# A gated feed-forward layer through tanh instead of SiLU, with a new order of the flow's steps

## The chip, the core and the metric

The kernel runs on one core of one Trainium2 chip. The metric is the time on the device in microseconds (us) of one execution; the figure for the kernel before is the median of three runs. A core has five engines that run at the same time and meet only at semaphores: PE (matrix multiplication, with a separate row for its weight loads), DVE (elementwise work and reductions), ACT (activation functions, copies, scaling), POOL (elementwise work and index-driven transfers) and SP, which here only issues transfers. Each engine works through its own instructions in the order in which the program gives them. PE writes to PSUM, a small memory of eight banks; DVE and ACT can read PSUM, POOL can't.

## What is computed

Eight batches of 512 tokens with 128 features pass through eight layers of attention, each followed by a feed-forward layer. The first half has experts that are chosen per token. The last four pairs of layers are the flow (called "stream" in the code) that this change touches: two attention layers and a feed-forward layer of kind `l2f`, twice, then the same with `l3f`; the last attention layer is a "hybrid" with a small router. Cut to what the change touches:

```
def ffn(x, w_gate, w_up, w_down):            # _L2_ffn_ref and _L3_ffn_ref
    gate = fp4_linear(x, w_gate)
    y = fp4_linear(x, w_up)
    h = jax.nn.silu(gate) * y
    return fp4_linear(h, w_down)             # h is quantised in blocks of 16

# in _L3_attn_b_ref
    logits = jax.nn.silu(route_in @ router_w1) @ router_w2 + router_b2
```

Here silu(g) = g * sigmoid(g). The hidden width of this layer is 352. Every other attention layer of the flow is causal softmax attention with 16 heads of 8 features; the softmax is taken with ACT's Exp.

## The kernel before

**The flow.** `stream` runs the four pairs of layers over eight batches, so 32 passes, numbered v = 0 to 31; pass v belongs to layer v // 8 and batch v % 8. The work of a pass is cut into steps with short names. Their order is one long written-out list of 237 entries, `STREAM`. An entry such as `V0:5` means: in round i, do step V0 of pass i - 5. So each round works on up to seven passes at once, each in another phase. `in_order` (L1806 and after) walks the list once per round; it leaves one empty place between the causal layers and the hybrid ones, and there are 32 + 1 + 6 = 39 rounds, the first and last ones only partly filled. A step that a pass does not have (the hybrid steps H, I, J, K in a causal layer, the steps m, x, w in a hybrid one) is left out. The kernel is built with manual scheduling: the instructions of each engine stand in the order in which the steps issue them, and a step issues to several engines.

**The feed-forward steps** are in `ffn_parts`. F0 to F8 normalise, quantise and transpose the input. V0 and V1 each compute the gates of two tiles of 128 tokens (L1382) into `ps`, a pair of PSUM banks from the pool `p_sc` with tag `sc`. S0 and S1 apply SiLU to such a pair on ACT (L1398) and write `sg` to SBUF. U0 to U3 compute the "up" product of one tile (L1382 again) into one bank. y0 to y3 multiply (L1407, DVE): h = sg * up, 128 x 352. z, D, C, A, M with a number quantise h: `scales` is a reduction and three short DVE instructions (L2420 to L2427), `divide` is on POOL, `cut` on ACT, `put` two dependent DVE instructions (L2446, L2447) for tiles 0 and 2 and three POOL instructions for tiles 1 and 3, `multiply` on POOL. n0 to n3 transpose h (L1415), N0 to N3 multiply with the down weights (L1424), E0 to E3 add to x (L1428).

**What shares the buffers.** `p_sc` has two pairs of banks. The attention scores take them too: each step x of `exp_parts` allocates a pair, has four (or two) matmuls written to it (L1093) and an Exp on ACT (L1103) that reads it; there are 24 such steps in a causal pass. In a hybrid pass the steps Ka to Kc use the pairs. The pool `p_b` has four single banks, for everything else: "up", the row-maximum products `mx` of the m steps (L1009, L1012, reduced on DVE in L1024), transposes, accumulators, the reduction result `amax`.

**Activation tables.** ACT evaluates Exp, SiLU, Gelu and Sqrt from tables; before an activation whose function is not in the set that is loaded stands an ACT_TABLE_LOAD. In the flow of the kernel before, such loads stand before L1398 (SiLU) and before the next Exp, in the causal layers L1103 and in the hybrid ones L1645 or others, and before the router's SiLU (L1537).

**The router** of the hybrid layer is in `hybrid_parts`: He (`route`) writes two small products into one bank, Hf (`hidden`) applies SiLU to 64 values on ACT, Hg (`at_landmarks`) reads the other part of the bank on DVE, Hh (`logits`) is a matmul of the hidden values, Hi (`biased`) adds the bias on DVE.

Of the kernel before, what the change touches and what calls it, by code (L numbers as in the profile page):

```python
# [25 lines left out]
AF = mybir.ActivationFunctionType  # L26
ALU = mybir.AluOpType
# [3 lines left out]
B, S, D, H, HD = 8, 512, 128, 16, 8  # L31
NT = S // P
EXPERTS, HID = 8, 512
FF = 352
# [48 lines left out]
class Net:  # L83
# [1094 lines left out]
    def stream(self, layers, back):  # L1178
# [3 lines left out]
        nc, a = self.nc, self.a  # L1182
        tile_pool = self.tc.tile_pool
        with tile_pool(name="flow_fix", bufs=1) as fix, tile_pool(name="flow", bufs=2) as pool, tile_pool(
# [182 lines left out]
            def ffn_parts(v, w, rows, cols, ffn_w, rope, eps, post):  # L1367

                b, box = v % B, {}
                gu, dn = ffn_w[:, 0 : 2 * FF], ffn_w[:, 2 * FF : 2 * FF + 3 * P].rearrange("p (c n) -> p c n", c=3)  # L1370
                xn = self.xnb(b)
                stats, shift, apply = self.norm_three(xn, self.xb(b))
                q = self.quantize_part(pool, xn.rearrange("p t d -> p (t d)"), S, "qx", 1)

                def turn():
                    box["xT"] = pool.tile([P, S], F32, tag="xT", name="xT", bufs=3)
                    self.transposed(box["xT"], xn, act=True)

                parts = {f"F{k}": f for k, f in enumerate((stats, shift, apply) + q + (turn,))}

                def wide(k, t, out):
                    nc.tensor.matmul(  # L1382
                        out[:, 0:FF],
                        lhsT=box["xT"][:, t * P : (t + 1) * P],
                        rhs=gu[:, k * FF : (k + 1) * FF],
                        start=True,
                        stop=True,
                    )


                def gates(i):
                    ps = box["ps", i] = self.sc()
                    for j in range(2):
                        wide(0, 2 * i + j, ps[:, j, :])

                def silu(i):
                    sg = box["sg", i] = pool.tile([P, 2, FF], F32, tag="sg", name="sg")
                    nc.scalar.activation(sg, box.pop(("ps", i))[:, :, 0:FF], AF.Silu)  # L1398

                def up(t):  # L1400
                    ps = box["up", t] = self.bank("up")
                    wide(1, t, ps)

                def product(t):
                    h = box["h", t] = pool.tile([P, FF], F32, tag="h", name="h", bufs=3)
                    sg = box["sg", t // 2][:, t % 2, :]
                    nc.vector.tensor_tensor(h, sg, box.pop(("up", t))[:, 0:FF], ALU.mult)  # L1407
                    box["q", t] = self.quantize_part(pool, h, FF, "qh", 2, t in (1, 3))

                def narrow_turn(t):  # L1410
                    h = box.pop(("h", t))
                    hT = box["hT", t] = pool.tile([P, 3, P], F32, tag="hT", name="hT")
                    pt = self.bank("m")
                    for c, (at, r) in enumerate(CH):
                        nc.tensor.transpose(pt[0:r, c * P : (c + 1) * P], h[:, at : at + r], self.ident)  # L1415
                    nc.scalar.copy(hT[:, 0:2, :], pt[:, 0 : 2 * P].rearrange("p (c n) -> p c n", c=2))
                    r = CH[2][1]
                    nc.scalar.copy(hT[0:r, 2, :], pt[0:r, 2 * P : 3 * P])

                def narrow(t):  # L1420
                    hT = box.pop(("hT", t))
                    o = box["o", t] = self.bank("av")
                    for c, (_, r) in enumerate(CH):
                        nc.tensor.matmul(o[:, 0:P], lhsT=hT[0:r, c, :], rhs=dn[0:r, c, :], start=c == 0, stop=c == 2)  # L1424

                def add(t):
                    x = self.xb(b)[:, t, :]
                    nc.vector.tensor_tensor(x, x, box.pop(("o", t))[:, 0:P], ALU.add)  # L1428
# [52 lines left out]
    def hybrid_parts(self, pool, b, weights, rows):  # L1481


        nc = self.nc
# [5 lines left out]
        wo, land, r2 = w[:, 929:1057], w[0:64, 1057:1185], w[0:64, 1185:1188]  # L1490
        scale = 32**-0.5
        xn = self.xnb(b)
        box, tiles = {}, {}
        stats, shift, apply = self.norm_three(xn, self.xb(b))

        def small(n, tag, bufs=2):
            return pool.tile([P, n], F32, tag=tag, name=tag, bufs=bufs)
# [28 lines left out]
            nc.vector.tensor_reduce(box["route"], box["xT"], AX.X, ALU.add)  # L1526

        def route():
            ps = box["r"] = self.bank("m")
            nc.tensor.matmul(ps[0:64, 0:1], lhsT=r1, rhs=box.pop("route"), start=True, stop=True)  # L1530
            nc.tensor.matmul(
                ps[0:1, 64:128], lhsT=box["xT"][:, S - 1 : S], rhs=landT, start=True, stop=True, skip_group_check=True
            )

        def hidden():
            hid = box["hid"] = small(1, "hhid")
            nc.scalar.activation(hid[0:64], box["r"][0:64, 0:1], AF.Silu, scale=1.0 / S)  # L1537

        def at_landmarks():

            t = box["at"] = small(72, "hat")
            nc.vector.tensor_copy(t[0:1, 0:64], box["r"][0:1, 64:128])
            nc.vector.tensor_reduce(t[0:1, 64:65], t[0:1, 0:64], AX.X, ALU.max, negate=True)
            nc.vector.tensor_scalar(t[0:1, 64:65], t[0:1, 64:65], D**-0.5, None, ALU.mult)

        def logits():
            ps = box["r"] = self.bank("m")
            nc.tensor.matmul(ps[0:1, 0:3], lhsT=box.pop("hid")[0:64], rhs=r2, start=True, stop=True)

        def biased():  # L1550
            t = box["lg"] = small(8, "hlg")
            nc.vector.tensor_tensor(t[0:1, 0:3], box.pop("r")[0:1, 0:3], rows[0:1, 256:259], ALU.add)
            nc.vector.tensor_reduce(t[0:1, 4:5], t[0:1, 0:3], AX.X, ALU.max, negate=True)

        def exponentials():
# [203 lines left out]


    STREAM = """
        Kd0:3 n2:6 x312:4 E1:6 Jc:4 m302:3 m220:3 x302:4 Jd:4 F5:5 t2:4 pv:2 d2:4 m221:3 Ka2:3 sk:2 x000:3 Ie:2
        F6:5 F7:5 m301:3 mg:1 x012:3 Je:4 M3:6 Ib:2 w3:4 m312:3 c3:4 m311:3 rv:2 x111:3 m320:3 Ke0:3 He:2 Kc3:3
        x010:3 m332:3 Kb2:3 Jf:4 t3:4 d3:4 st:1 Kf0:3 F8:5 N2:6 m321:3 Hk:3 m300:3 x011:3 Kd1:3 V0:5 Kc2:3 Hl:3
        Hg:2 E2:6 Jg:4 Hf:2 m330:3 m201:3 Hm:3 S0:5 Jh:4 aT:4 m200:3 sh:1 U1:5 n3:6 Kd2:3 Kd3:3 Ke1:3 g1 x001:3
        Kf1:3 x002:3 y1:5 U0:5 z1:5 y0:5 m231:3 l1:2 po:4 z0:5 N3:6 ap:1 Ka0:2 Jk:4 m322:3 E3:6 Ke2:3 bi:4 D1:5
        If:2 o0:4 Hn:3 D0:5 x101:3 Hh:2 m310:3 m210:3 l0:2 f1:3 x100:3 Ha:1 m110:2 o1:4 Ho:3 w0:3 C1:5 C0:5 h1:3
        m122:2 c0:3 V1:5 i1:3 A0:5 m112:2 Ji:4 A1:5 m131:2 m101:2 g0 S1:5 o2:4 T:1 Kb0:2 m130:2 Kf2:3 U2:5 y2:5
        Ke3:3 t0:3 o3:4 Ic:2 z2:5 Jj:4 Kc0:2 Hb:1 d0:3 M0:5 Jl:4 o4:4 x112:3 m111:2 ad:4 pq:1 m000:2 x110:3 D2:5
        l2:2 m020:2 pk:1 Hi:2 Ka3:2 Id:2 rq:1 m132:2 x102:3 M1:5 Pq:1 rk:1 U3:5 l3:2 Kf3:3 x201:3 Jm:4 Rq:1  # L1770
        m022:2 m030:2 x200:3 F0:4 y3:5 n0:5 w1:3 z3:5 C2:5 D3:5 c1:3 x210:3 A2:5 m002:2 x202:3 m031:2 M2:5 Ka1:2
        m011:2 n1:5 Hc:1 m032:2 x211:3 x212:3 m102:2 C3:5 m021:2 F1:4 sq:1 m100:2 Kb1:2 N0:5 A3:5 E0:5 F2:4
        m010:2 x300:3 m012:2 x301:3 Kb3:2 Hj:2 m212:2 m121:2 m001:2 Pk:1 m120:2 f0:2 t1:3 w2:3 d1:3 Rk:1 h0:2
        F3:4 m230:2 c2:3 i0:2 Hd:1 x310:3 m211:2 Ja:3 F4:4 Ia:1 Jb:3 x311:3 Kc1:2 m222:2 m331:2 m202:2 N1:5
        m232:2
# [913 lines left out]
```

## Time and profile before

| what | value |
|---|---|
| median of three runs | 3313.77 us (3310.12 to 3315.57) |
| the profiled execution | 3321.43 us, of this the core's span 3319.6 us |
| mean granted TensorE clock | 0.923 |
| ACT_TABLE_LOAD in the trace | 138, each 1283 ns |
| SiLU in the feed-forward layers (L1398) | 64 instructions of 128 x 704, 756 ns mean |
| product h = sg * up (L1407) | 128 instructions of 128 x 352 |
| Exp of the scores (L1103) | 832 instructions, 923 ns mean |
| from 1740.0 to 1838.2 us (flow fills) | 98.2 us; PE busy 88.55, DVE 78.70, ACT 62.46 |
| from 1838.2 to 2858.7 us (20 full causal rounds) | 1020.5 us, some 51 us each |
| from 2858.7 to 3052.3 us (change to the hybrid layer) | 193.6 us; PE busy 164.01, DVE 154.31, ACT 137.17 |
| from 3052.3 to 3319.6 us (hybrid rounds and the end) | 267.3 us |

The stages were taken from the start of the first SiLU (1838.2 us), which begins the feed-forward work of pass 0, and of every second one after it. Times inside the trace are in us from the start of the span. In the profile, lines of a group give: source line, engine, operation, output <- input, shapes, count, then busy time in us and the mean of one instruction in ns, then the idle time of the engine just before such instructions and what ended it. In the list of stages each engine has its busy time in us and, in brackets, its number of instructions; PEclk is the granted clock. The chain of waits is one path through the trace, followed back from the last instruction: at each step to what released the instruction, or to the one before it on its engine. A line of it has start, length, engine, tile and source line. ACT with a line and no tile is there a table load. Matmuls overlap one another and their ends are modelled, so a PE that is 98% busy may still have room.

### The profile page before, as it was taken

The page shows a single profiled execution, that of the slowest core. Times are in us where ns is not written, and L with a number is a line of the kernel's source. Part 1 is how long each engine was busy: PE and PEld are TensorE (multiplying, and loading weights), DVE is VectorE, ACT ScalarE, POOL GpSimd, SP SyncE. Part 2 cuts the span into 40 slices and gives each one's busy share as a digit, 9 for nine tenths or more (in the row PEclk, how much of TensorE's full clock was granted, in tenths as well). Part 3 has the DMA queues.
Part 4 walks back from the last instruction along what each step waited for, and adds up shares of the span by engine and source line. Part 5 has one row for each costly group of instructions (what it writes and reads, how often), then busy time and mean ns, then how long its engine had stood idle before and what let it go on. Part 6 is the DMA issues. An engine that isn't in the chain of part 4 may idle for free.

```text
span 3319.6 us, 65455 instructions
## 1 busy us (share of the span) xinstructions
PE 2823.0 (85%) x21824; PEld 1887.0 (57%) x21824; DVE 2521.8 (76%) x6837; ACT 2112.6 (64%) x4192; POOL 1852.6 (56%) x2476
## 2 busy tenths in 40 slices
PE   7783899999795867788748999999999999888886
PEld 4582753333295757767725566665656666555554
DVE  7844768998545696475337999989899999778895
ACT  5533478787643543566416778888888788676663
POOL 3355623431155652553335886677787777576676
PEclk9986999999897978899869999999999999998898
DMA  2023322221022300221232221111211111100000
GB/s 89 13 64 79 98 56 66 65 65 55 8 68 59 114 26 23 68 56 50 59 103 79 68 71 70 65 67 66 74 63 63 63 66 65 63 2 1 7 7 13
DMA packets 134774, 187.36 MB, mean 56 GB/s; under 512 B 20292, under 2 KB 103364, under 8 KB 134444
## 3 DMA queue, kind: packets, MB, share of 16 engines
q1 hardware_dynamic: 118348, 150.46, 13.6%
q0 software_dynamic: 14080, 28.86, 4.2%
q10 hardware_dynamic: 2016, 3.85, 0.5%
q8 instruction: 181, 2.97, 0.4%
q14 instruction: 149, 1.22, 0.1%
HBM read 128.81 MB, written 54.30 MB: 55 GB/s over the span
## 4 chain that ended last, share of the span: by engine, by line
PE 50%; DVE 28%; ACT 6%; DMA 6%; issue 5%; POOL 4%; SPq 1%; DVEq 0%; ACTq 0%; POOLq 0%
PE sc L826 6%; PE av L843 6%; PE av L1124 6%; PE mx L1012 6%; PE sc L1093 6%; DVE pm L1024 4%; DMA k<-d 3%; DVE nm L1031 2%; DVE bnst L205 2%; DVE bnmv L206 2%; PE m L1227 2%; PE av L1424 2%; ACT e L1103 2%; PE mx L1009 2%; PE sc L1382 1%
## 5 line engine op out<-in xcount | busy, mean ns | idle before, releaser
L1103 ACT ACTIVATE e<-sc 128x1024 f32<-128x1024 f32 (+1 forms) x832 | 739.3, 923 | 172.0 <-PE sc L1093 101.7
L1024 DVE TENSOR_REDUCE pm<-mx 128x4 f32<-128x512 f32 (+1 forms) x1152 | 629.6, 595 | 93.7 <-PE mx L1012 89.0
L1012 PE MATMUL mx<-k,q 126*128 126x512 bf16 (+3 forms) x2048 | 547.3, 321 | 44.5 <-DMA k<-d 34.9
L1093 PE MATMUL sc<-q,k 128*128 128x512 bf16 (+3 forms) x2048 | 446.4, 320 | 10.6 <-ACT e L1103 8.2
L1106 POOL TENSOR_SCALAR_AFFINE_SELECT e<-e 128x256 f32<-128x256 f32 x768 | 298.5, 409 | 205.7 <-ACT e L1103 201.0
L1124 PE MATMUL av<-e,vaug 128*32 128x512 f32 (+3 forms) x4096 | 369.1, 482 | 1.3 <-ACT e L1103 0.8
L1031 DVE TENSOR_REDUCE nm<-mx 128x1 f32<-128x512 f32 x512 | 329.2, 684 | 46.0 <-PE mx L1012 44.2
L806 POOL DMA_INDIRECT xg<-xd,srci x248 | 243.6, 982 | 211.7 <-DVE srci L799 107.2
L1012 PEld LDWEIGHTS <-q 126*128 126x128 bf16 x2048 | 197.6, 98 | 247.9 <-issue 167.8
L843 PE MATMUL av<-moe_w,h 128*128 x1984 | 266.9, 278 | 15.0 <-ACT xgT L820 4.5
L826 PE MATMUL sc<-xgT,w1c 128*128 128x128 f32 x1984 | 276.8, 285 | 2.4 <-ACT e L1103 2.4
L1009 PE MATMUL mx<-maskbf,identbf 128*128 128x128 bf16 (+1 forms) x1152 | 265.8, 238 | 10.0 <-DVE pm L1024 6.7
L892 POOL DMA_INDIRECT got<-yd,posi x192 | 199.8, 1041 | 133.1 <-issue 56.5
L826 PEld LDWEIGHTS sc<-xgT,w1c 128*128 128x128 f32 x1984 | 256.4, 201 | 14.5 <-ACT e L1103 4.6
L1093 PEld LDWEIGHTS <-k 128*128 128x128 bf16 x2048 | 183.1, 98 | 139.6 <-issue 56.8
L843 PEld LDWEIGHTS av<-moe_w,h 128*128 128x128 f32 x1984 | 243.1, 193 | 27.6 <-issue 8.0
L187 POOL TENSOR_SCALAR rstd<-bnmv 128x4 f32<-128x4 f32 x152 | 48.3, 318 | 373.8 <-DVE bnmv L206 365.6
L251 ACT ACTIVATE xn<-x,ln_shift,rstd 128x128 f32<-128x128 f32 x480 | 197.9, 489 | 67.0 <-DVE ln_shift L246 67.0
L814 DVE COPY w1c<-moe_w 128x516 f32 x248 | 117.2, 473 | 129.4 <-issue 32.4
L1124 PEld LDWEIGHTS av<-e,vaug 128*32 128x32 f32 x4096 | 107.7, 110 | 172.1 <-issue 145.4
L829 ACT ACTIVATE h<-sc 128x512 f32<-128x512 f32 x156 | 93.2, 598 | 166.0 <-PE sc L826 161.2
L262 PE MATMUL m<-ident,xn 128*128 128x128 f32 x480 | 85.4, 297 | 95.0 <-ACT xn L251 67.9
(427 smaller groups left out, 6386.7 us busy)
## 6 DMA issues: line engine op xcount, KB each, us to landing
q<-d SPq DMA_DIRECT2D x128, 288.0 KB
k<-d SPq DMA_DIRECT2D x384, 96.0 KB
d<-thirds SPq DMA_DIRECT2D x48, 384.0 KB
yd<-y SPq DMA_DIRECT2D x248, 64.0 KB
xd<-xn SPq DMA_DIRECT2D x32, 256.0 KB
d<-thirds SPq DMA_DIRECT2D x48, 128.0 KB
moe_w<-in_moe_w SPq DMA_DIRECT2D x8, 516.0 KB
moe_w<-in_moe_w SPq DMA_DIRECT2D x8, 512.0 KB
```

The costliest lines, as they stand in the source:

```text
L806: nc.gpsimd.indirect_dma_start(xg[i], None, s["xd"], bass.IndirectOffsetOnAxis(ap=srci[:, i : i + 1], axis=0))
L826: nc.tensor.matmul(ps[:, cols], lhsT=w1c[i][:, cols], rhs=xgT[i], start=True, stop=True)
L843: nc.tensor.matmul(ps[:, 0:P], lhsT=hid[i][:, c * P : (c + 1) * P], rhs=w2[:, bass.ds(e + c * P, P)], start=c == 0, stop=c == 3,)
L892: nc.gpsimd.indirect_dma_start(got[b][k][:, i, :], None, s["yd"], bass.IndirectOffsetOnAxis(ap=s["posi"][:, j : j + 1], axis=0))
L1009: nc.tensor.matmul(out, lhsT=self.identbf, rhs=mask, start=True, stop=False, skip_group_check=True)
L1012: nc.tensor.matmul(s[:, col : col + n], lhsT=q[:, t, :], rhs=key[:, 0 : n // P, :], start=not causal, stop=True, skip_group_check=True,)
L1024: nc.vector.tensor_reduce(box["pm"][:, h, at : at + n // P], s[:, 0:n].rearrange("p (k n) -> p k n", n=P), AX.X, ALU.max,)
L1031: nc.vector.tensor_reduce(box["nm"][:, u, h : h + 1], s, AX.X, ALU.max, negate=True)
L1093: nc.tensor.matmul(s[:, jj, col : col + n], lhsT=key[:, t, :], rhs=q[:, at // P : (at + n) // P, :], start=True, stop=True,)
L1103: nc.scalar.activation(e, s[:, :, 0:wide], AF.Exp, scale=scale)
L1106: nc.gpsimd.affine_select(out=e[:, :, col : col + P], in_=e[:, :, col : col + P], pattern=[[0, 2], [1, P]], compare_op=ALU.is_ge, fill=0.0 ...
L1124: nc.tensor.matmul(acc[g][32 * j : 32 * j + 32, at : at + n], lhsT=vaug[:, t, first : first + 32], rhs=pair[j // 2][:, j % 2, col : col + ...
```

## The change

Three things, all in the flow.

1. The gate. sigmoid(g) = (1 + tanh(g/2)) / 2, so silu(g) * u = (1 + tanh(g/2)) * u * g / 2. S0 and S1 now write tanh(g/2). The product step has two DVE instructions in place of one: h = (sg + 1) * up, then h = (h * 0.5) * gate, where gate is the PSUM pair of step V. The second reads what the first wrote. The PSUM pair was last read by S before; now it is last read by the second product of the odd tile, so by y1 or y3.
2. The router. `hidden` writes tanh of half the mean, `logits` has a DVE instruction of 64 x 1 ahead of its matmul that makes (1 + tanh) * g, and `biased` scales by 0.5/S while it adds the bias. The bank that `route` writes is named `r0` and is read by `logits` too.
3. The list STREAM is a new one: the same steps in another sequence, some with another lag (`E1:6` becomes `E1:5`, `Kd0:3` becomes `Kd0:2`, `mg:1` becomes `mg`, among others). The largest lag is 6 in both, so there are 39 rounds in both.

```diff
                 def silu(i):
                     sg = box["sg", i] = pool.tile([P, 2, FF], F32, tag="sg", name="sg")
-                    nc.scalar.activation(sg, box.pop(("ps", i))[:, :, 0:FF], AF.Silu)
+                    nc.scalar.activation(sg, box["ps", i][:, :, 0:FF], AF.Tanh, scale=0.5)
...
                     sg = box["sg", t // 2][:, t % 2, :]
-                    nc.vector.tensor_tensor(h, sg, box.pop(("up", t))[:, 0:FF], ALU.mult)
+                    gate = box["ps", t // 2][:, t % 2, 0:FF]
+                    nc.vector.scalar_tensor_tensor(h, sg, 1.0, box.pop(("up", t))[:, 0:FF], ALU.add, ALU.mult)
+                    nc.vector.scalar_tensor_tensor(h, h, 0.5, gate, ALU.mult, ALU.mult)
+                    if t % 2:
+                        del box["ps", t // 2]
...
-            ps = box["r"] = self.bank("m")
+            ps = box["r0"] = self.bank("m")
...
-            nc.scalar.activation(hid[0:64], box["r"][0:64, 0:1], AF.Silu, scale=1.0 / S)
+            nc.scalar.activation(hid[0:64], box["r0"][0:64, 0:1], AF.Tanh, scale=0.5 / S)
...
         def logits():
+            hid = box.pop("hid")
+            nc.vector.scalar_tensor_tensor(hid[0:64], hid[0:64], 1.0, box["r0"][0:64, 0:1], ALU.add, ALU.mult)
             ps = box["r"] = self.bank("m")
-            nc.tensor.matmul(ps[0:1, 0:3], lhsT=box.pop("hid")[0:64], rhs=r2, start=True, stop=True)
+            nc.tensor.matmul(ps[0:1, 0:3], lhsT=hid[0:64], rhs=r2, start=True, stop=True)
...
-            nc.vector.tensor_tensor(t[0:1, 0:3], box.pop("r")[0:1, 0:3], rows[0:1, 256:259], ALU.add)
+            logit = box.pop("r")[0:1, 0:3]
+            nc.vector.scalar_tensor_tensor(t[0:1, 0:3], logit, 0.5 / S, rows[0:1, 256:259], ALU.mult, ALU.add)
```

Of the list, the stretch around the gates, first as it was and then as it is:

```
... N2:6 m321:3 Hk:3 m300:3 x011:3 Kd1:3 V0:5 Kc2:3 Hl:3 Hg:2 E2:6 Jg:4 Hf:2 m330:3 m201:3 Hm:3 S0:5 Jh:4 aT:4
    m200:3 sh:1 U1:5 n3:6 Kd2:3 Kd3:3 Ke1:3 g1 x001:3 Kf1:3 x002:3 y1:5 U0:5 z1:5 y0:5 ...

... rv:2 m312:3 Ib:2 Ke0:3 Kf0:3 V0:5 m331:3 S0:5 m321:3 Hd:2 Kd2:3 x002:3 sh:1 He:2 U0:5 aT:4 Jg:4 x111:3 U1:5
    Kc3:3 If:2 y0:5 z0:5 y1:5 Jh:4 Ke1:3 po:4 Ka0:2 Ke2:3 D0:5 Hf:2 Jk:4 bi:4 z1:5 o0:4 V1:5 ...
    ... S1:5 ... x110:3 ... U2:5 ... y2:5 ... U3:5 n0:5 z2:5 x112:3 N3:6 o3:4 y3:5 ...
```

The loads and stores of an attention pass move as well: `l1:2` (four transfers on SP) stands 65 entries after `sk:2` (a store on SP) in the old list and 9 after it in the new one; `g1`, a pair of index-driven fetches on POOL, moves from place 71 to place 10, `l0:2` from 100 to 109, `l2:2` from 149 to 125, `l3:2` from 162 to 173, `sq:1` from 195 to 183. Between V0 and the product that frees its pair stand two score steps in the new list (x002, x111), between V1 and y3 two more (x110, x112); in the old list no score step stands between V0 and S0 or between V1 and S1.

More of the change, by code (lines that the diff above doesn't have):

```diff
@@ L1536, in hidden @@
             hid = box["hid"] = small(1, "hhid")
-            nc.scalar.activation(hid[0:64], box["r"][0:64, 0:1], AF.Silu, scale=1.0 / S)
+            nc.scalar.activation(hid[0:64], box["r0"][0:64, 0:1], AF.Tanh, scale=0.5 / S)
         def at_landmarks():
             t = box["at"] = small(72, "hat")
-            nc.vector.tensor_copy(t[0:1, 0:64], box["r"][0:1, 64:128])
+            nc.vector.tensor_copy(t[0:1, 0:64], box["r0"][0:1, 64:128])
             nc.vector.tensor_reduce(t[0:1, 64:65], t[0:1, 0:64], AX.X, ALU.max, negate=True)
@@ L1761 @@
     STREAM = """
[L1762 to L1775, printed above, removed]
+        w3:4 F5:5 F6:5 sk:2 Ie:2 F7:5 m302:3 m320:3 c3:4 Ka3:3 g1 m210:3 l1:2 x001:3 m230:3 Hm:3 x000:3 m311:3
+        Je:4 m301:3 Kc1:3 m202:3 Kb3:3 Ia:2 x100:3 m211:3 M3:6 m232:3 x011:3 m322:3 t3:4 Jf:4 x012:3 d3:4 st:1
@@ new lines @@
+        F8:5 m332:3 pv:2 m300:3 Kd1:3 m330:3 x010:3 rv:2 m312:3 Ib:2 Ke0:3 Kf0:3 V0:5 m331:3 S0:5 m321:3 Hd:2
+        Kd2:3 x002:3 sh:1 He:2 U0:5 aT:4 Jg:4 x111:3 U1:5 Kc3:3 If:2 y0:5 z0:5 y1:5 Jh:4 Ke1:3 po:4 Ka0:2 Ke2:3
+        D0:5 Hf:2 Jk:4 bi:4 z1:5 o0:4 V1:5 m201:3 m102:2 ap:1 Hh:2 g0 Kf1:3 w0:3 Ha:1 C0:5 D1:5 A0:5 M0:5 Hg:2
+        Kd3:3 S1:5 Ji:4 Hi:2 Jj:4 c0:3 o1:4 n3:6 m132:2 C1:5 T:1 A1:5 M1:5 x110:3 Kf2:3 f1:3 Jl:4 m120:2 l0:2
+        Kb0:2 U2:5 Kc0:2 o2:4 Jm:4 y2:5 h1:3 i1:3 U3:5 n0:5 z2:5 x112:3 N3:6 o3:4 y3:5 l2:2 E3:6 Ka1:2 m110:2
@@ new lines @@
+        o4:4 m130:2 x101:3 m121:2 Ke3:3 Hj:2 Kf3:3 m101:2 x102:3 pk:1 n1:5 pq:1 ad:4 Ka2:2 rk:1 D2:5 z3:5 mg
+        t0:3 d0:3 Pq:1 rq:1 m112:2 Rq:1 m111:2 x200:3 Hb:1 m011:2 D3:5 x211:3 w1:3 C2:5 F0:4 c1:3 x212:3 x201:3
+        A2:5 m122:2 m100:2 m001:2 x311:3 Kb1:2 m032:2 Hc:1 l3:2 F1:4 m012:2 m010:2 x210:3 Ja:3 m002:2 Jb:3
+        m031:2 x202:3 sq:1 N1:5 C3:5 E1:5 m131:2 N0:5 E0:5 t1:3 d1:3 m021:2 Pk:1 m022:2 Kb2:2 M2:5 Hk:2 Rk:1
+        F2:4 Hn:3 A3:5 x310:3 m030:2 x300:3 m020:2 m000:2 w2:3 F3:4 Jc:3 m212:2 f0:2 c2:3 Ho:3 n2:5 Jd:3 m231:2
@@ L1776 @@
+        F4:4 x301:3 m220:2 Kd0:2 t2:3 m222:2 x302:3 h0:2 d2:3 i0:2 Ic:2 Id:2 N2:5 Hl:2 E2:5 m310:2 x312:3 Kc2:2
+        m221:2 m200:2
     """
```

## The prediction

> **What bounds the kernel now.** The changed lines L1398 and L1407 run from 1838 us on, so the stages of the profile come first, then the idle time of the engine that the change loads, then the chain of waits.
>
> ```profile
> core 0: us, PE busy (x) PEld busy (x) DVE busy (x) ACT busy (x) POOL busy (x), PEclk, DMA share, GB/s
> 1838.20:2858.70 1020.50, 993.94 (x8283) 627.16 (x8282) 933.27 (x2610) 828.43 (x1334) 774.00 (x1220) 1.00 0.19 67
> 2657.20:2707.60 50.40, 49.96 (x418) 31.68 (x417) 46.55 (x129) 40.37 (x65) 36.83 (x60) 1.00 0.18 66
> 3088.30:3128.70 40.40, 33.41 (x166) 21.66 (x166) 34.50 (x100) 25.37 (x77) 27.32 (x32) 0.87 0.02 7
> ```
>
> The first line is all 20 full causal rounds, then one of them, then a hybrid round. DVE is busy 933.27 of 1020.5 us (91%), ACT 81%, and in the hybrid round DVE is the busiest engine (85%). PE's 97% has modelled ends in it, so I ask whether DVE waits for it:
>
> ```profile
> DVE pm L1024 <- PE mx L1012: 59.1, 98, 1.9
> DVE x L1428 <- PE av L1424: 19.6, 11, 4.2
> DVE h L1407 <- PE up L1382: 12.2, 7, 3.2
> ```
>
> These are DVE's three largest waits on another engine's compute from 1838.2 us to the end; they sum to 90.9 us in 1481.4. In 20 causal rounds the maxima wait some 2.5 to 3 us a round. So DVE and PE set the pace together, DVE with some 5% in hand. ACT, from which the change takes work, is third:
>
> ```profile
> L1103 ACT ACT_TABLE_LOAD x54 | 69.3, 1283 | 12.5 <-PE sc L1093 8.9 <-DMA k<-d 2.2 <-PE av L1124 0.5
> L1398 ACT ACT_TABLE_LOAD x45 | 57.7, 1283 | 0.8
> L1407 DVE TENSOR_TENSOR h<-sg,up 128x352 f32<-128x352 f32 x128 | 65.0, 507 | 17.4 <-PE up L1382 12.2 <-PE m L1415 2.7 <-ACT sg L1398 2.0
> L2446 DVE SCALAR_TENSOR_TENSOR qh_a<-cut,qh_a 128x352 f32<-128x352 f32 x64 | 32.9, 513 | 6.5 <-ACT cut L2437 6.5
> L2447 DVE SCALAR_TENSOR_TENSOR qh_a<-cut,qh_a 128x352 f32<-128x352 f32 x64 | 33.6, 525 | 2.2
> ```
>
> The reader sees the load that goes (1283 ns) and two rows that the new products copy: L2446 and L2447 are two dependent instructions of this kind and size, each with one operand in PSUM.
>
> **The change, part by part.**
>
> *The table loads.* The instructions of the built programs show 138 loads before and 33 after; 33 is also the number of loads in the trace ahead of 1740 us. So the flow loses 105 (45 before L1398, 8 before L1537, the other 52 on the way back to Exp): 105 x 1.283 = 134.7 us of ACT, four loads (5.1 us) a causal round. What is that worth? Most loads lie beside other work: ACT has some 10 us of idle time a causal round (51.0 - 41.4). I count along the chain of waits from 1838 us on: 10 of the 105 loads stand in it, 12.8 us. One of them:
>
> ```profile
> 2307.42 0.85 DVE ln_shift L246
> ...
> 2309.96 1.28 ACT L1103
> 2311.25 1.51 ACT e L1103 x2
> 2312.76 0.49 ACT nat L1236
> 2313.30 0.86 PE up L1382 x2
> ```
>
> I take -12.8 us; the ends are 0 (another chain beside it, as long) and -30 (if all the idle time of L1103's Exp behind PE, which is late for lack of score pairs, shrinks by a half). The Trainium skill ("ScalarE: Activation LUTs", What ACT_TABLE_LOAD costs) prices a switch at about 2.66 us, the load and a drain of some 1.38 us; by that the chain's ten loads would be worth 26.6 us and the sum below would end at 3325.7 us. The row speaks against the drain: 45 loads before L1398 had 0.8 us of idle time ahead of them in all.
>
> *The second product.* 128 DVE instructions more. The price is read from how such pairs follow each other:
>
> ```profile
> 2679.08 0.49 DVE L1407 TENSOR_TENSOR h<-sg,up 128x352 f32<-128x352 f32 x1
> 2679.60 0.53 DVE L2420 TENSOR_REDUCE amax<-h 128x22 f32<-128x352 f32 x1
> ...
> 2680.62 0.51 DVE L2446 SCALAR_TENSOR_TENSOR qh_a<-cut,qh_a 128x352 f32<-128x352 f32 x1
> 2681.17 0.53 DVE L2447 SCALAR_TENSOR_TENSOR qh_a<-cut,qh_a 128x352 f32<-128x352 f32 x1
> ```
>
> From the start of the first of a dependent pair to the start of the second it is 0.55 us, so DVE gets 128 x 0.55 = 70.4 us more, 2.2 us a round. That nearly uses up what DVE has in hand in the maxima's waits. Of the 128 products 70 stand in the chain from 1838 us on, so on the path as it is it costs 70 x 0.55 = 38.5 us. The ends are 0 (each falls into a wait of DVE) and 70.4. The first product, an add and a multiply in place of a multiply, is L2446's 513 ns against L1407's 507: nothing. Tanh on ACT has SiLU's shape; no row shows it in this kernel, and I take SiLU's 756 ns (bounds by the copies and Exp per element nearby: within 10%, 64 x 0.08 = 5 us of ACT either way, under its idle time).
>
> *The gate's PSUM pair.* It is held until the second product of the odd tile. Queued behind it on PE are score steps, two in each hold by the new list (x002 and x111; x110 and x112), which must share the other pair; behind PE's wait stand the maxima that DVE needs. x111 waits for x002's Exp (0.60 us for 128x512); U0 and the transposes aT stand between, 0.59 + 0.44 us by the chain's lines. V1 waits for x111's Exp (about 1.02 us); U1 and po stand between, 0.59 + 0.95 us. I take 0, and to the other side one uncovered Exp of 0.8 us in each of 48 causal holds: 38 us.
>
> *The router.* 8 DVE instructions of 64 x 1, nearest row 181 ns (L2423, 128 x 22), and a hand-over to PE: at most 8 x 0.4 = 3 us, beside the hybrid round's other batches. The bank `r0` is held to Hg or Hh, over some 35 entries where before it was some 23; I take 0, bound 5 us.
>
> *The sequence.* It moves every engine's work, and the list alone doesn't tell what that gives. What can be read: SP's loads. `l1` was 24 entries ahead of the first m step that needs it and is now 67; the shortest lead is now 47 entries, 10 us at 51 us for 237 entries, against the 9.8 and 6.9 us of the two such transfers that stand in the chain (the rounds there are 1.4 us longer than their neighbours): worth up to 3 us. `l1` now stands right behind the store `sk` on SP and waits there for its landing (2.8 us in the chain); the next SP steps come 100 entries later. `g1` goes ahead of POOL's masks, a pair of fetches of about 1 us each, in eight rounds: POOL has 25% idle. For the rest I take 0, with half of DVE's 59.1 us of waits for maxima as the bound on both sides, 30 us.
>
> *Sum.* 38.5 - 12.8 = +25.7 us. The profiled execution took 3321.43 us, 1.83 of it around its span of 3319.6; with 25.7 it would be 3347.1. It lay 7.66 us above the median of the runs, so the median goes from 3313.77 to 3339.5 us, +0.8%. DVE's floor agrees: 933.3 + 20 x 2.2 = 977 of a causal stage of 1020.5 us, 96%, where the stages shown have 91 to 92%.
>
> **The rivals.**
>
> *Faster: DVE's waits go faster than its work comes.* ACT is relieved by 5.1 us a round, Exp frees the score pairs sooner, PE gets ahead and the maxima never wait. For it: ACT's 81%, and the new list is free to use the room. Against: in the round of 2657 us the chain is nearly all PE and holds no load. If three quarters of the 59.1 us of waits fall away (44 us), the time is 3339.5 - 44 = 3295 us. It decides from 32 us on: 25.7 to cancel the cost and 6.6 to be told from no change.
>
> *Slower still: the gate's pair is late.* The holds cost what was bounded above, 38 us, and DVE's waits for the maxima grow as PE stands: 3339.5 + 38 = 3378 us.
>
> *No change.* The 2.2 us a round fall into DVE's 2.5 to 3 us of waits and into the hybrid round's gaps, and the loads pay the rest: 3314 us.
>
> That the change doesn't do what it says, because tanh and Exp might need different tables, is excluded by the 33 loads.
>
> **How the numbers follow.** The forecast (3321 to 3360) has 0.43, slower still 0.22, no change 0.11, faster 0.24. What a measurement of this kernel can tell from no change is about 0.2%, 6.6 us. Faster 0.24, within 0.2% 0.11, slower 0.65. The time is that of the forecast, 3339.5. The range reaches down to the faster rival with 5 us to spare (3290) and up past the late pair (3392), which leaves out a tenth on either side. The forecast and the late pair alone would be 3321 to 3392.
>
> **What would show it.** Right: no table load after 1740 us; a group of 128 new products near 515 ns; DVE above 94% in full causal rounds that are 51.5 to 53 us long; hybrid rounds up by 1 to 2 us; DVE's waits for the maxima down, but by less than 30 us. The late pair: PE at L1093 or L1382 waiting for DVE's product. Wrong: causal rounds under 50.5 us with DVE at 97%, which would say that DVE's waits were ACT's doing and the new list could remove them.

## The result, and the profile after

The changed kernel took 3340.92 us (median of 4 runs, 3336.04 to 3347.15) beside 3314.67 us for the kernel before (4 runs, 3310.12 to 3316.92). The ratio is 1.0075, 95% interval 1.0059 to 1.0091: slower by 0.75%, 25 us (the two medians are 26.3 us apart). The forecast was 3339.5 us.

The table of stages of the changed kernel, cut where the first tanh of pass 0 starts (1843.70), at the start of the hybrid rounds (2928.20) and where the last two rounds begin (3264.00):

```profile
0.00:1843.70 1843.70, 1459.00 (x11412) 1022.35 (x11420) 1224.90 (x3185) 998.24 (x2108) 780.22 (x886) 0.90 0.23 62
1843.70:2928.20 1084.50, 1044.48 (x8599) 659.62 (x8681) 1024.82 (x2816) 767.55 (x1308) 800.78 (x1268) 1.00 0.18 65
2928.20:3264.00 335.80, 280.56 (x1484) 183.99 (x1484) 283.00 (x834) 194.10 (x597) 217.13 (x267) 0.86 0.01 4
3264.00:3345.40 81.40, 52.39 (x241) 36.85 (x239) 48.27 (x142) 26.98 (x77) 50.34 (x58) 0.77 0.05 14
```

The same four stages of the kernel before:

```profile
0.00:1838.20 1838.20, 1456.80 (x11417) 1017.35 (x11418) 1225.48 (x3183) 999.84 (x2108) 778.20 (x881) 0.89 0.23 62
1838.20:2919.00 1080.80, 1043.82 (x8685) 658.83 (x8684) 977.76 (x2735) 864.99 (x1391) 804.07 (x1273) 0.99 0.19 66
2919.00:3242.30 323.30, 272.68 (x1487) 174.99 (x1487) 277.73 (x794) 221.98 (x622) 220.81 (x266) 0.88 0.02 4
3242.30:3319.60 77.30, 49.70 (x240) 35.83 (x238) 40.85 (x129) 25.75 (x74) 49.48 (x58) 0.80 0.05 14
```

The columns are the stretch, its length, then PE, PEld, DVE, ACT and POOL with busy time and number of instructions, the granted clock, and DMA. The stage of the causal rounds got only 3.7 us longer (1084.5 against 1080.8), although DVE has 47 us more in it; ACT has 97 us less. The hybrid stage got 12.5 us longer, the end 4.1, and the stretch ahead, in which the flow fills, 5.5.

The groups of the changed lines, and the two largest groups of the table loads that are left:

```profile
L1409 DVE SCALAR_TENSOR_TENSOR h<-h,sc 128x352 f32<-128x352 f32 x128 | 66.7, 521 | 4.4
L1408 DVE SCALAR_TENSOR_TENSOR h<-sg,up 128x352 f32<-128x352 f32 x128 | 65.0, 508 | 7.6 <-PE up L1382 7.0 <-ACT sg L1398 0.5
...
L829 ACT ACT_TABLE_LOAD x13 | 16.7, 1283 | 1.8 <-PE sc L826 1.6
L1103 ACT ACT_TABLE_LOAD x10 | 12.8, 1283 | 0.7 <-PE av L1124 0.5
```

The second product takes 521 ns, the first is as dear as the one before it was. Of the 138 loads 33 are left, all ahead of the first tanh (the last starts at 1742.2 us). In the list of waits, DVE's in the causal stage read:

```profile
DVE pm L1024 <- PE mx L1012: 17.5, 67, 0.7
DVE x L1432 <- PE av L1428: 3.1, 15, 0.2
```

The maxima waited 59.1 us before and wait 17.5 us now. So DVE's new work has gone where its waits were: it is 93 to 97% busy in the first 19 causal rounds. Read alone, this says: tanh freed ACT, ACT freed PE, and DVE's waits paid for most of the product. The experiments show another cause.

### The profile page after: what moved, and what is told of

It is laid out like the page before. It is cut to its first block, busy times and chain, and to the rows that moved or that the text cites. A ratio compares the mean times of both kernels' runs of the same rounds, so it can differ in the third digit from the quotient of the medians.

```text
span 3345.4 us, 65533 instructions
## 1 busy us (share of the span) xinstructions
PE 2836.4 (85%) x21731; PEld 1902.8 (57%) x21824; DVE 2581.0 (77%) x6973; ACT 1986.9 (59%) x4087; POOL 1848.5 (55%) x2476
## 4 chain that ended last, share of the span: by engine, by line
PE 47%; DVE 34%; DMA 5%; issue 5%; ACT 4%; POOL 4%; SPq 0%; DVEq 0%; ACTq 0%; POOLq 0%
PE av L1124 8%; DVE pm L1024 7%; PE sc L826 6%; PE av L843 6%; PE mx L1012 5%; PE sc L1093 5%; DVE nm L1031 2%; DMA k<-d 2%; PE mx L1009 2%; DVE bnst L205 2%; PE av L1428 2%; DVE bnmv L206 2%; DVE h L1409 2%; DVE amax L2427 2%; DVE h L1408 1%
## 5 line engine op out<-in xcount | busy, mean ns | idle before, releaser
L1103 ACT ACTIVATE e<-sc 128x1024 f32<-128x1024 f32 (+1 forms) x832 | 741.9, 924 | 230.8 <-PE sc L1093 134.4
L1024 DVE TENSOR_REDUCE pm<-mx 128x4 f32<-128x512 f32 (+1 forms) x1152 | 621.4, 591 | 46.0 <-PE mx L1012 44.2
L1093 PE MATMUL sc<-q,k 128*128 128x512 bf16 (+3 forms) x1955 | 429.9, 317 | 8.5 <-ACT e L1103 4.8
L1093 PEld LDWEIGHTS <-k 128*128 128x128 bf16 x2048 | 182.3, 98 | 123.6 <-issue 45.1
L191 POOL TENSOR_TENSOR rstd<-rstd,mhalf 128x4 f32<-128x4 f32 x152 | 159.4, 1049 | 12.7
```

Of the source, the lines that this page charges most:

```text
L1024: nc.vector.tensor_reduce(box["pm"][:, h, at : at + n // P], s[:, 0:n].rearrange("p (k n) -> p k n", n=P), AX.X, ALU.max,)
L1093: nc.tensor.matmul(s[:, jj, col : col + n], lhsT=key[:, t, :], rhs=q[:, at // P : (at + n) // P, :], start=True, stop=True,)
L1103: nc.scalar.activation(e, s[:, :, 0:wide], AF.Exp, scale=scale)
```

## The experiments

Runs were made on other chips too. In those of e1 to e11 the kernel before took 3448.5 to 3457.9 us, since the part ahead of the flow is longer there (the first SiLU or tanh starts at 1963 to 1983 us, not at 1838 or 1844), and in that of e12 3318.8 us; so each run is given as a ratio to the kernel before on its own chip, and its excess in us is that ratio less 1, times that kernel's median.

The change has two halves that can be exchanged: the operations (tanh, second product, held pair) and the sequence (the list STREAM). Four runs take them apart.

**e1_old_list: the new operations in the old sequence.** Tile 1's product comes before tile 0's there, so the pair is freed behind the later one:

```diff
-        w3:4 F5:5 F6:5 sk:2 Ie:2 F7:5 m302:3 m320:3 c3:4 Ka3:3 g1 m210:3 l1:2 x001:3 m230:3 Hm:3 x000:3 m311:3
...
+        Kd0:3 n2:6 x312:4 E1:6 Jc:4 m302:3 m220:3 x302:4 Jd:4 F5:5 t2:4 pv:2 d2:4 m221:3 Ka2:3 sk:2 x000:3 Ie:2
...
-                    if t % 2:
+                    if ("q", t ^ 1) in box:
                         del box["ps", t // 2]
```

> The tanh products and the router's tanh with the list of before (the pair of gates is freed behind the later one of its two products, which in this list is y0 or y3). My theory (the operations cost 25.7 us, the sequence nothing): 3340 us. Rival, sequence: the operations cost all of DVE's 70.4 us less the chain's loads of 12.8 us, 3372 us, and the new list won some 30 us back. Rival, late pair: the old list puts no score step ahead of the pair's release with the hold in mind, so 3378 us or more, with PE at L1093 or L1382 waiting for DVE's product.

**e2_new_list: the kernel before (SiLU, one product) in the new sequence.**

```diff
-        Kd0:3 n2:6 x312:4 E1:6 Jc:4 m302:3 m220:3 x302:4 Jd:4 F5:5 t2:4 pv:2 d2:4 m221:3 Ka2:3 sk:2 x000:3 Ie:2
...
+        w3:4 F5:5 F6:5 sk:2 Ie:2 F7:5 m302:3 m320:3 c3:4 Ka3:3 g1 m210:3 l1:2 x001:3 m230:3 Hm:3 x000:3 m311:3
...
```

> SiLU and one product as before, with the new list alone (the router's bank is named r0 as in the change, since its second reader comes later in this list). My theory: 3315 us, within 7 us of before. Rival, sequence: 3285 us, as much faster as e1 is slower than 3340. A third possibility: the new list is worse in the hybrid rounds (321 us of 2919 to 3242 us before) whatever the operations, and better in the causal ones.

**e3_one_product and e4_three_products: the changed kernel with one product fewer, and one more.** First e3, then e4:

```diff
                     nc.vector.scalar_tensor_tensor(h, sg, 1.0, box.pop(("up", t))[:, 0:FF], ALU.add, ALU.mult)
-                    nc.vector.scalar_tensor_tensor(h, h, 0.5, gate, ALU.mult, ALU.mult)
```

```diff
                     nc.vector.scalar_tensor_tensor(h, h, 0.5, gate, ALU.mult, ALU.mult)
+                    nc.vector.scalar_tensor_tensor(h, h, 2.0, gate, ALU.mult, ALU.mult)
```

> The changed kernel without its second product: h is (1 + tanh) * up, the factor gate / 2 is left out, and so the pair of gates is free after the tanh. By the chain of before (70 of 128 products, 38.5 us): 3302 us. By the chain of the changed kernel (103 of 128 second products stand in it, 53.8 us): 3287 us. If the second product were hidden: 3341 us. If the held pair cost something beside the product: below 3270 us.

> The changed kernel with a third product, h * 2 * gate, behind the second (h has one factor more than the reference). By the chain of the changed kernel: 3341 + 54 to 57 = 3396 us. If DVE sets the pace throughout, every one of 128 x 0.55 us counts: 3411 us. If DVE still had room: under 3370 us.

Measured: e1 1.0283 (1.0259 to 1.0308), e2 1.0113 (1.0086 to 1.0139), e3 0.9936 (0.9912 to 0.9959), e4 1.0263 (1.0239 to 1.0286). Each half alone is dearer than both together. The new operations cost 98 us in the old sequence; the new sequence costs 39 us with the old operations; together they cost 25. The causal and the hybrid stage took 1080.8 and 323.3 us before; the same two stages of e1, then of e2:

```profile
1975.80:3108.80 1133.00, 1045.40 (x8558) 660.66 (x8681) 1019.97 (x2819) 766.93 (x1308) 808.65 (x1272) 0.99 0.18 63
3108.80:3463.10 354.30, 286.99 (x1488) 185.37 (x1489) 292.52 (x829) 195.90 (x602) 220.56 (x268) 0.84 0.01 4
1980.70:3076.10 1095.40, 1040.63 (x8602) 655.92 (x8684) 986.38 (x2732) 869.87 (x1391) 802.66 (x1268) 1.00 0.18 65
3076.10:3427.20 351.10, 288.56 (x1477) 190.35 (x1480) 272.01 (x793) 235.00 (x629) 217.97 (x266) 0.83 0.01 4
```

e1 is 52 us longer in the causal stage and 31 in the hybrid one, e2 15 and 28. The steady causal round of e1 in the table of stages, and DVE's waits in it:

```profile
2833.20:2886.20 53.00, 49.99 (x412) 31.74 (x416) 48.57 (x133) 35.67 (x60) 37.05 (x60) 1.00 0.17 63
```

```profile
DVE pm L1024 <- PE mx L1012: 2.6, 5, 0.9
DVE h L1408 <- PE up L1382: 0.4, 1, 0.4
```

The round took 50.40 us before. ACT is relieved as in the changed kernel (35.67 us against 40.37), the product is there, and DVE's waits for maxima are still 2.6 us (2.5 before). So neither the relief of ACT nor DVE's need removes them; the sequence does. It does so with SiLU too: in the causal stage of e2 they are 26.4 us.

What e2 pays in its causal stage is to be looked for in its chain of waits there. The parts "ACT L1103" and "ACT L1398" without a tile are table loads:

```profile
by line: PE av L1124 14.2%; PE mx L1012 12.8%; PE sc L1093 11.1%; PE mx L1009 6.7%; PE av L1424 5.4%; DVE pm L1024 5.1%; PE m L1227 5.0%; ACT e L1103 4.4%; ACT L1103 3.6%; issue 2.5%; ACT L1398 2.5%; PE m L1141 2.4%; PE av L1337 2.2%; PE sc
```

6.1% of 1095.4 us is 67 us of loads on the path, where I had counted 12.8 us in the kernel before, from its first SiLU to its end. But what stands in the chain is not the price. e2 and e3 differ by the loads (and by the form of the product and the router): 0.0177, 61 us in all, of which 40.0 us lie in the causal stage (1055.4 us in e3) and 21.5 us in the hybrid stage (329.6 us in e3). Nor are the loads the same ones: e2 has 152, 14 more than the kernel before.

**e5_after_beside** is the changed kernel again, on the chip of the next three runs, to see whether e1's excess is the chip's.

> The changed kernel itself, beside the next three runs. If the excess of e1 (+2.83% with the old sequence) is an interaction of operations and sequence, this kernel stays near its earlier ratio of 1.0075 (1.005 to 1.010). If it comes from the chip on which e1 to e4 ran, which took 3457.9 us for the kernel before where the first took 3314.7, this ratio goes up with them, to 1.02 or more.

It gave 1.0061 (1.0041 to 1.0081), as on the first chip. So the new sequence is worth 0.0283 - 0.0061 = 2.2% under the new operations, 77 us. The next runs take e1's 98 us apart.

**e6_hold_alone: the held pair without the second product**, in the old sequence with SiLU.

```diff
-                    nc.scalar.activation(sg, box.pop(("ps", i))[:, :, 0:FF], AF.Silu)
+                    nc.scalar.activation(sg, box["ps", i][:, :, 0:FF], AF.Silu)
...
                     nc.vector.tensor_tensor(h, sg, box.pop(("up", t))[:, 0:FF], ALU.mult)
+                    seen = self.small([P, 1], "seen")
+                    nc.vector.tensor_copy(seen, box["ps", t // 2][:, t % 2, 0:1])
+                    if ("q", t ^ 1) in box:
+                        del box["ps", t // 2]
```

> The kernel before (SiLU, one product, old sequence), with one thing added: at each product DVE copies one column of the gate (128x1) from PSUM, so that a pair of banks with gates stays taken until both its products, as in the change. 128 copies, at some 0.06 us each (by the 0.04 to 0.06 us of the 128x22 L2434) are 8 us of DVE. Theory H, that the held pair costs PE its other pair for the scores: in e1 a steady causal round has 1.8 us of PE waiting at L1093 for an exponential (L1103), twice a round, and that returns here: 21 rounds by 1.8 us, +38 us in the causal stage, ratio 1.010 to 1.015. Rival D, that DVE's time for the second product makes e1's excess: ratio 1.000 to 1.003.

1.0249 (1.0231 to 1.0267), 86 us, of which the copies can be 128 x 0.151 us = 19 us. That is more than either theory gave. In the order of time, one hold of a steady round of e6 (start, duration, engine, line; in brackets the idle time before and its releaser):

```profile
2853.82 0.76 ACT L1398 ACTIVATE sg<-sc 128x704 f32<-128x704 f32 x1
...
2855.65 1.28 ACT L1103 ACT_TABLE_LOAD   x1
...
2856.95 1.02 ACT L1103 ACTIVATE e<-sc 128x1024 f32<-128x1024 f32 x1
2858.02 0.59 PE L1093 MATMUL sc<-q,k 128*128 128x256 bf16 x2 [2.52 <-ACT e L1103]
...
2858.40 1.38 PE L1382 MATMUL up<-fp_w,xT 128*128 128x352 f32 x2
...
2859.82 0.52 DVE L1407 TENSOR_TENSOR h<-sg,up 128x352 f32<-128x352 f32 x1 [3.18 <-PE up L1382]
```

PE's scores (L1093) need a pair. One is held for the product that is still to come, the other is being read by the Exp, and that Exp stands behind a table load. PE waits 2.52 us. The product that would free the held pair waits for its "up", which stands on PE behind those scores: DVE waits 3.18 us. The old sequence has two score steps between the "up" steps of a pass's first hold, three between those of its second, and two more ahead of the second's last product; the new one has one, none and one. The waits of the causal stage of e6, and then of e1:

```profile
PE sc L1093 <- ACT e L1103: 78.1, 64, 4.6
```

```profile
PE sc L1093 <- ACT e L1103: 38.3, 42, 2.1
```

In the kernel before they were 1.8 us, and in the changed kernel they are not among the largest waits. In e1 the load is gone from the Exp's way, and the same waits are half as long. In the lines of e6's rounds, three of the four from 2798.70 us on have a granted clock of 0.97, as this one, where the kernel before has 1.00:

```profile
2853.80:2908.70 54.90, 51.14 (x411) 32.57 (x416) 47.19 (x134) 40.57 (x66) 37.00 (x60) 0.97 0.16 60
2908.70:2962.10 53.40, 49.63 (x411) 31.73 (x416) 46.91 (x133) 40.51 (x64) 36.91 (x60) 1.00 0.17 60
```

In the first of these PE is busy 51.14 us with work that takes 49.96 us in the kernel before. The second has the same waits at L1093 (3.4 us), a clock of 1.00, and is 1.5 us shorter. So a round with the lower clock costs a second time; that the hold lowers the clock is likely, not shown.

**e7_copied_old: no hold, by a copy of the gates.**

```diff
+                    ps = box.pop(("ps", i))[:, :, 0:FF]
+                    gt = box["gt", i] = pool.tile([P, 2, FF], F32, tag="gt", name="gt", bufs=1)
+                    nc.scalar.copy(gt, ps)
...
-                    gate = box["ps", t // 2][:, t % 2, 0:FF]
+                    gate = box["gt", t // 2][:, t % 2, :]
```

> e1 (new operations, old sequence) with the gates copied from PSUM to SBUF by ACT right behind the tanh (64 copies of 128x704, about 0.75 us each as the tanh, 48 us of ACT, in place of the loads' 135), and the second product reading the copy; to make room sg and the copy have one buffer each. DVE's work is that of e1. Theory H: PE's waits at L1093 for exponentials (1.8 us in a steady round) go, the ratio falls from 1.028 to about 1.015, steady rounds of 53.0 us to about 51.2. Rival D: it stays within 1.025 to 1.031, since DVE's 0.52 us per product are all there.

1.0291 (1.0267 to 1.0314): a miss for the theory of the hold, and what the rival, DVE's time, was to give. PE's waits at L1093 are gone from the list as expected, but the time is e1's. One reason is the second product, which now reads SBUF twice:

```profile
L1412 DVE SCALAR_TENSOR_TENSOR h<-h,gt 128x352 f32<-128x352 f32 x128 | 88.7, 693 | 9.3 <-ACT attnT L264 0.5
```

It takes 693 ns in place of 521, 22 us more in all. It is not the whole reason: in the round from 2840.60 us its four products take 2.3 us together, 0.2 more than in e1, and the round is 52.9 us (53.0 in e1). So the run shows that the waits for the pair can be removed, and that this gains little in a steady round of e1. It does not price the hold, because it changed other things too, the operands of the product and the copies on ACT.

**e9_product_alone: the second product without the hold**, reading PSUM, in the old sequence with SiLU.

```diff
-                    nc.vector.tensor_tensor(h, sg, box.pop(("up", t))[:, 0:FF], ALU.mult)
+                    up = box.pop(("up", t))[:, 0:FF]
+                    nc.vector.tensor_tensor(h, sg, up, ALU.mult)
+                    nc.vector.scalar_tensor_tensor(h, h, 1.0, up, ALU.mult, ALU.max)
```

> The kernel before (SiLU with its loads, old sequence, the pair of gates freed behind the SiLU) with a second product on DVE that reads the up bank again from PSUM, h = max(h, up): 128 more instructions of some 0.52 us (the second product of the change), 67 us of DVE, and no held pair. e1 (both) gave 1.0283, e6 (the hold, with 128 copies of 0.151 us) 1.0249. If each of the two is enough by itself, and they overlap: 1.018 to 1.028. If the hold makes the excess and DVE's time has room (90 to 94% busy in causal rounds, PE 96 to 99%): 1.000 to 1.010. If they add: 1.003 to 1.010 too, by the difference of e1 and e6.

1.0188 (1.0164 to 1.0211): 65 us for 66.6 us of products (128 at 521 ns). Practically all of it is on the path. PE's waits, then DVE's, in a steady round of e9:

```profile
PE av L1426 <- DVE h L1409: 0.6, 1, 0.6
PE m L1417 <- DVE qh_a L2449: 0.6, 1, 0.6
PE m L1227 <- DVE h L1409: 0.4, 1, 0.4
PE mx L1009 <- DVE qh_minus L2429: 0.2, 1, 0.2
```

```profile
DVE pm L1024 <- PE mx L1012: 2.6, 5, 0.9
```

The 1.8 us that PE waits for the later products and their followers stand against 0.4 us before. And the 2.6 us that DVE waits for maxima stand as they were. That idle time of DVE was no room for the product: it lies at other places of the queue than the product does, and the sequence has fixed both.

**e10_loads_alone: the loads alone.**

```diff
-                    nc.scalar.activation(sg, box.pop(("ps", i))[:, :, 0:FF], AF.Silu)
+                    nc.scalar.activation(sg, box.pop(("ps", i))[:, :, 0:FF], AF.Tanh, scale=0.5)
```

> The kernel before with tanh for SiLU in the flow and in the router, and nothing else: one product, old sequence; the (1 + ...) times the gate is left out. 105 table loads go. Step 1 of the prediction put this at -12.8 us (0 to -30): ratio 0.996 (0.991 to 1.000). Rival: the loads are worth as much with the old sequence as with the new one, where e3 and e2 (0.9936 and 1.0113) put them at 1.8%: ratio 0.982.

0.9953 (0.9931 to 0.9976): 16 us for 134.7 us of loads. The steady round goes from 50.40 to 50.30 us, ACT's time in it from 40.37 to 35.45.

**e12_new_no_hold: the changed kernel without the hold.** The second product reads "up" again and the pair is freed behind the tanh:

```diff
-                    nc.scalar.activation(sg, box["ps", i][:, :, 0:FF], AF.Tanh, scale=0.5)
+                    nc.scalar.activation(sg, box.pop(("ps", i))[:, :, 0:FF], AF.Tanh, scale=0.5)
...
+                    nc.vector.scalar_tensor_tensor(h, h, 0.5, up, ALU.mult, ALU.max)
```

> The changed kernel with its new sequence, in which the pair of gates is freed behind the tanh and the second product reads the up bank again instead of the gate (the output is not the reference's); DVE's work is the same. Beside the kernel before, the changed kernel gave 1.0061 and e3 (no second product, no hold) 0.9936. If the new sequence has taken away the hold's price, and the 1.25% between them are DVE's time alone: 1.004 to 1.009, and steady causal rounds of 51.8 us as in the changed kernel. If the held pair still costs there: 0.996 to 1.002.

1.0088 (1.0061 to 1.0115), with rounds of 51.8 us. In the new sequence the hold costs nothing that these runs can tell (beside the first chip's 1.0075 the intervals leave room for some 0.2%, 6 us).

The steady rounds side by side, each the 17th, from the start of a SiLU or tanh to the second one after it (the first 20 rounds of the old sequence, in the order of the table, have means of 51.0, 50.7, 53.0, 54.9 and 53.5 us):

| kernel | sequence | round, us | DVE busy | ACT busy | DVE's waits for maxima |
|---|---|---|---|---|---|
| before | old | 50.40 | 46.55 | 40.37 | 2.5 |
| e10, loads gone | old | 50.30 | 46.41 | 35.45 | 2.6 |
| e9, product | old | 52.60 | 48.50 | 40.33 | 2.6 |
| e6, hold | old | 54.90 | 47.19 | 40.57 | 3.2 |
| e1, all three | old | 53.00 | 48.57 | 35.67 | 2.6 |
| e2, SiLU | new | 52.30 | 47.60 | 40.59 | 1.4 |
| e3, loads gone | new | 50.50 | 47.64 | 35.75 | 1.4 |
| after, all three | new | 51.80 | 49.49 | 35.82 | 0.7 |

**Two attempts to beat both, e8_pool_new and e11_pool_second.** e3 shows what there would be to gain: 0.9936. Both put a product on POOL, from a copy of the gate that ACT makes; e8 ahead of DVE's product, e11 behind it. Their edits to the product, e8 first:

```diff
+                    nc.scalar.activation(sg, sg, AF.Copy, scale=0.5, bias=0.5)
+                    nc.gpsimd.tensor_tensor(sg, sg, box["gt", t // 2][:, t % 2, :], ALU.mult)
```

```diff
-                    nc.vector.scalar_tensor_tensor(h, h, 0.5, gate, ALU.mult, ALU.mult)
+                    nc.gpsimd.tensor_tensor(h, h, gate, ALU.mult)
```

> A version meant to keep the gain alone, with the new sequence: ACT writes tanh, a copy of the gate and 0.5*tanh+0.5 (128x704 each), POOL multiplies the two (128 tensor_tensor of 128x352, 0.79 us each by L2438: 101 us more of POOL, which is 70 to 80% busy in causal rounds), and DVE makes one product from SBUF and PSUM as before the change. e3, with the second product left out, gave 0.9936. If DVE's second product is what the change pays, the ratio is 0.993 to 0.998. If POOL's and ACT's added work comes into the path (ACT 128 by 0.75 us = 96 us in place of 135 us of loads, but ahead of each product), it is 1.000 or more.

> A version meant to beat both: the changed kernel with the second product on POOL (128 tensor_tensor of 128x352 in SBUF, 0.79 to 0.93 us each), ACT copying 0.5 times the gate from PSUM to SBUF behind the tanh (64 of some 0.75 us), one buffer each for sg and the copy, and in the sequence the first reduction of tile 0's quantization (z0) set some steps later, so that DVE doesn't wait for POOL there; for the other three tiles other work lies between already. If what e8 lost (1.0637) was DVE waiting for POOL ahead of the product (225.6 us at its L1413), this has it no more, and the ratio is 0.994 to 1.000, near e3's 0.9936. If POOL's queue (67 to 80% busy in causal rounds, 7 points more now) makes the rest wait, it is above 1.006.

1.0637 (1.0608 to 1.0666) and 1.0519 (1.0492 to 1.0547). In both DVE waits for POOL. Of e11's waits from 1980 to 3060 us:

```profile
DVE amax L2428 <- POOL h L1412: 109.1, 37, 4.4
...
PE mx L1009 <- DVE qh_minus L2435: 84.7, 37, 4.0
```

The reduction behind the product stands too early in DVE's queue, PE's next maxima too early behind the quantization, and one moved entry did not mend that. A sequence made for these operations was not tried. No version here that computes the reference beats the kernel before.

## Why the prediction was right, and where it was not

The time (3339.5 against 3340.9 us) and the side were right, and that the time came out so close was luck: terms of the sum were off, two of them by more than their bounds, and the errors cancel. What a term is worth also depends on which half is exchanged first, so the table has both ways:

| term | predicted, us | measured, operations first, us | measured, sequence first, us |
|---|---|---|---|
| table loads | -12.8 (0 to -30) | -16 (e10) | -61 (e3 less e2, which has 14 loads more) |
| second product | +38.5 (0 to 70.4) | +65 (e9) | +43 (e5 less e3) |
| held pair | 0 (to 38) | +49: e1's 98, less the two above | 0 (e12) |
| sequence | 0 (30 either way) | -77 (e5 less e1) | +39 (e2) |
| sum | +25.7 | +21 (e5), +25 (first chip) | +21 (e5) |

*The table loads* were right in the old sequence, and the rival that has ACT's relief turn into speed (3295 us) falls with e10. With the new sequence they are worth 61 us, beyond the range. The count along the chain came near the price in one sequence and not in the other, where it gives 67 us for a stage that gets 40 us shorter without loads; so it was no sure way to the size.

*The second product* was mis-sized by its step "of the 128 products 70 stand in the chain from 1838 us on, so on the path as it is it costs 70 x 0.55". The duration was right (521 ns). A chain shows which products end last now. It does not show how little room the others have: in a round in which PE is 99% busy, a product that is half a microsecond late finds PE waiting. In the old sequence nearly all 128 counted. The price on the new sequence, from e3 to e5, is 0.0125, 43 us, not far from the 38.5, and a third product (e5 to e4) costs 0.0202, 70 us, its whole duration again.

*The held pair* was taken at 0 by reading the new list, in which U1 and one score step lie between; e12 shows that right. For the operations as such it was wrong: in the old sequence the hold is worth 49 us beside the product and up to 86 us alone, more than the bound of 48 x 0.8 us. The bound counted one uncovered Exp a hold. It left out the table load ahead of that Exp, the product that waits for the PE which it blocks, the rounds with a lower clock, and the hybrid rounds. In the causal rounds the sign that I named, PE waiting for DVE's product, was the wrong one too: the wait shows as PE at L1093 waiting for an Exp, the reader of the other pair. But by the same subtraction stage by stage (e9 1120.4 and 337.0 us, e10 1073.7 and 316.1) only some 20 of the 49 us lie in the causal stage; some 24 lie in the hybrid stage, and there the named sign is the largest of e1's waits of PE, at a line that I had not named, the hybrid scores, which take a pair too:

```profile
PE sc L1638 <- DVE h L1409: 19.8, 7, 4.0
```

That wait is in neither the kernel before nor the changed one.

*The sequence* was the step that failed most: "For the rest I take 0". Half of 59.1 us bounded it, and it took away 77 us with the new operations and added 39 with the old ones, both beyond that bound. DVE's waits for maxima fell by 41.6 us, more than the 30 named, but that is only a part of it: the list also took away the hold's waits.

*The signs.* DVE at 93 to 97% in the causal rounds and products of 521 ns came nearly as said. Of the first 19 causal rounds nine have the 51.5 to 53 us named; eight are shorter, five of them with 50.7 us shorter than before (51.3 to 52.7), and two are longer (53.3). Hybrid rounds are longer by 2.3 us on average (the five from 3062.3 us against the five from 3052.3), where 1 to 2 were named. A wait that the new sequence brings is among them, in the changed kernel's list of waits of PE from 3062.3 to 3264 us:

```profile
PE m L1619 <- DVE hgate L1603: 16.0, 5, 3.2
```

It is 15.5 us in e2 and in e3, so it is neither the product's nor the loads'. What the router's share is was not measured by itself, and how the costs of the hold, the product and the loads depend on each other, beyond the two ways of the table, stays open.

## What to carry to other kernels

In a kernel whose engines work through a written-out order, operations and order are one design: here each half of the change alone cost more (2.83% and 1.13%) than both together (0.75%), so a change of operations that is tried in the old order is not a verdict on it, and a prediction that sets "new order" at 0 has left out its largest term. An engine's idle time in a round is room for new work only where it lies at the new work's place in the queue; the wait that could have paid for the product stayed at 2.5 to 3.2 us a steady round until the order moved. A count of instructions along the chain of waits is a guess at their price, near in one order here and far off in the other. And a buffer that is held longer should be followed to what stands between its last reader and that reader's own inputs: in the causal rounds here the wait showed at the other buffer of the pool, under the name of an instruction that the change never touched.

## What the hardware showed that I had not expected

A product of 128 x 352 on DVE took 521 ns with one operand in PSUM, and 524 to 1501 ns, 693 on average, with both in SBUF (e7). The Trainium skill ("SBUF — State Buffer", SBUF: two separate sides) says that a DVE instruction with two SBUF inputs and a GpSimd instruction that reads SBUF exclude each other on a shared port. The trace agrees; two of these products, the second with the POOL instruction that starts beside it:

```profile
2353.33 0.53 DVE L1412 SCALAR_TENSOR_TENSOR h<-h,gt 128x352 f32<-128x352 f32 x1
2355.45 1.17 DVE L1412 SCALAR_TENSOR_TENSOR h<-h,gt 128x352 f32<-128x352 f32 x1
2355.45 0.79 POOL L2439 TENSOR_TENSOR qh_a<-h,qh_rc 128x352 f32<-128x352 f32 x1
```

The 38 products with no POOL instruction beside them took 524 to 527 ns, the 11 with L2439 alone beside them 751 to 1123 ns. Not every POOL instruction does this: 17 with L191 (128 x 4) alone took 524 to 536 ns. No run here took POOL's work away.

PE's granted clock was 1.00 in all 20 full causal rounds of the kernel before and 0.97 in ten of the first 20 of e6, in each of which PE has a wait of 2.52 us or more. No length of wait that decides this can be read from these runs: e6 has the same wait in rounds at 1.00 (from 2908.70 us), e1 has one of 2.1 us in a round at 1.00 (from 2560.50 us), and e9 has a round at 0.97 in which no wait of PE is above 1.0 us (from 2546.20 us).
